# Two pre-activation layers, eight images: residual tiles reused, projection order, correlation joined by four, compact last sums

## The chip, the cores and the metric

The kernel runs on one core of a Trainium2 chip. The metric is the device time of one execution in microseconds (us). The kernel before was run three times: 2642.22, 2646.41 and 2648.47, median 2646.41.

## The reference

Eight images of 768 channels and 32x32 tokens, fp32, pass through two layers. Each layer normalizes in 32 groups of channels and adds its result to its input.

```python
def _L0_conv_ref(x, W_qkv, W_proj, b_proj):          # 12 heads of 64
    qkv = swapaxes(x.reshape(B, C, N), 1, 2) @ W_qkv.T
    q, k, v = ...
    var_v = jnp.var(v, axis=-1, ddof=1, keepdims=True)
    var_k = jnp.var(k, axis=-1, ddof=1, keepdims=True)
    scores = var_v @ jnp.swapaxes(var_k, -2, -1) * scale
    out = softmax(scores, axis=-1) @ v
    return (out as tokens x C) @ W_proj.T + b_proj

def _L1_conv_ref(feature, conv_w, conv_b):
    norm = jnp.sqrt(jnp.sum(feature * feature, axis=1, keepdims=True))
    feat_n = feature / jnp.maximum(norm, 1e-12)
    feat_pad = pad feat_n by 3 on both sides
    corr = stack of sum(feat_pad[r:h+r, cc:w+cc] * feat_n, axis=1) for 28 offsets (r, cc)
    x = jnp.concatenate([feature, corr], axis=1)       # 768 + 28 channels
    return jnp.einsum('bchw,oc->bohw', x, conv_w) + conv_b

x = x + _L0_conv_ref(_gn(x), W_qkv, W_proj, b_proj)
x = x + _L1_conv_ref(_gn(x), conv_w, conv_b)
```

The queries are not needed: the scores are an outer product of two variances for each token. The 28 offsets lie on two diagonals, a row and a column of a 7x7 window.

## The kernel before

**Products.** The three large matrix products (keys and values, projection, convolution) go by a block scheme with seven products instead of eight, numbered p = 1 to 7: some multiply sums of blocks of the weights with sums of blocks of the data. A *unit* is one such product (g, p), for one third g of the output channels: 12 matmuls of 128x64 stationary and 512 wide in the projection and the convolution (class `Wide`, 21 units each), 384 wide in keys and values (`KeysValues`). `halves` (L337 is its matmul) issues two matmuls of 64 columns for each 128 rows. All matmuls are fp32, so the trace has two passes for each instruction, and shapes like `128*64` are the tile of the array that an instruction occupies. Products 1, 5 and 2 open an accumulator in PSUM and later products add to it: `Banks.begin` opens it in one of two banks tagged x or one of two tagged y (z products use the y banks), `close` hands it to VectorE, which adds bias and residual (`take`; `vector` is a helper, and all its work stands at L153).

**Operand sums** of the data for products 5, 6/3, 7 and 4 are made by VectorE (`TokenSums`): t1, t2, t4 for layer one's output `f`, t1o, t2o, t4o for the attention output (the `ots` tiles, in the trace named v).

**Attention** (`Attention`): for each of six pairs of heads, ScalarE computes exponentials (`ex`, L738), TensorE multiplies them with the values (`av`, L763; one step of eight matmuls, 16 for half a pair in the planned order), and the denominators come either from ScalarE's running sums or from VectorE's sums `acc` of the exponentials. In the second case a product with ones (`den`) adds over partitions: `sum_up` (L797) makes four sums at once, each in a quarter of the columns, and sends them through memory to be inverted; `sum_up_last`, for an image's last pair, uses 64 columns for each sum (L847), so that the sums already lie on all 64 partitions of a head; VectorE inverts them there in four pieces and multiplies `v` with the result (v<-v,acc).

**Correlation** (`Corr`): TensorE makes grams of `f` (L1101, `gr`), of which DMAs pick the needed diagonals; `scale` turns them (`ct`, through `turned`, L340) and stores them as rows; a gather reads the rows with their shifts into `cs`, where VectorE forms the 28 channels. The channels are split like the data into two halves and their difference. They enter the convolution as a short product that is added to a unit's accumulator: `Wide.join` (L1008), which takes two units at a time, the operands of the first at partitions 0 to 39, of the second at 64 to 103. Seven images have six such joins each; for the last image the parts are added separately.

**The loop** (L1449) makes nine passes. Pass b holds the attention of image b, the second half of its keys and values, and the grams and the convolution of image b-1, interleaved; then `project(b)`, the projection of image b with the statistics for layer two; then the first half of keys and values of image b+1.

**What sets the order.** The program is emitted in one order by a planner: a clock with modelled durations (KV_US, T_US, CORR_US, TAIL and the like), `later.after(us, job)` for due times, `later.after_dve` for due times behind VectorE, and `work_off`, which mixes units and attention steps. The order on each engine is fixed by that. Nearly all DMAs are issued from SyncE (SP) in that order; an issue that waits for a reader of its target holds up those behind it. Eight completion semaphores are used in turn, so a DMA also waits until the one eight places before it has landed. Weight tiles `wt` are fetched by `TStream` (L324) up to twelve ahead (HELD).

**Residuals.** `Conv.start` loads x1 (kept in memory) into a new tile of the xn kind (x<-x1d in the trace); `project` loads x into a new tile f (L1336: f<-in_x_dram), both in six parts of 512 KB while the units already run.

The projection starts with units (0,1), (1,1), (0,5), (1,5), then products 6 and 3, whose operand t2o needs the last pair of heads. At its start stand:

```python
for n, (us, _, unit) in enumerate(wide.units()):
    if n == 4:
        clock.wait(("ot", b, HP - 1), ready=ready)
```

Of the kernel before, what the change touches and what calls it, by code (L numbers as in the profile page):

```python
# [38 lines left out]
NCH = 2 * NA + 4  # L39
# [11 lines left out]
TAIL = 14.0  # L51
# [3 lines left out]
WARM = 36  # L55
# [12 lines left out]
SINGLE = ((2, 1), (2, 5), (2, 6), (2, 2), (2, 7), (2, 3), (2, 4))  # L68
ORDER = (1, 5, 6, 3, 7, 4, 2)
OPENING = PAIR[:2] + PAIR[-2:] + PAIR[2:-2]  # L70

# [87 lines left out]
def two_layers(ctx, tc, x, wkv, wproj, bproj, wconv, wcorr, bconv, out):  # L159
# [147 lines left out]
    class TStream:  # L307
        def __init__(self):
            self.keys = []
            for b in range(NB + 1):  # L310
                for kind in ["c"] * (b > 0) + ["p"] * (b < NB):
                    some = PAIR[:-2] if b == NB - 1 and kind == "c" else PAIR
                    self.keys += [(kind, g, p) for g, p in some + SINGLE]
            at = len(self.keys) - len(PAIR + SINGLE)
            self.keys[at:at] = [("c", g, p) for g, p in PAIR[-2:]]
            self.loaded, self.tiles = 0, []
# [25 lines left out]
    class Banks:  # L342
# [8 lines left out]
        def product(self, g, p, us, width, pairs, taken):  # L351
            self.close(*self.begin(g, p, width, pairs), us, taken)

        def begin(self, g, p, width, pairs, stop=True, between=None):
            bank = BANK[p]
            of = "x" if bank == "x" else "y"
            if p in FIRST:
                slot = of, self.count[of] % 2
                self.count[of] += 1
                self.finish(slot)  # L360
                clock.pass_time(max(self.free.get(slot, 0.0) - clock.now, 0.0))
                t = (xbank if of == "x" else ybank).tile([P, width], F32, tag=of, name=f"{bank}{self.count[of]}")
                self.open[g, bank] = slot, t
            slot, t = self.open[g, bank]
            self.finish(slot)
            clock.pass_time(max(self.free.get(slot, 0.0) - clock.now, 0.0))
            for k, (lhsT, rhs) in enumerate(pairs):
                halves(
                    t, lhsT, rhs, start=p in FIRST and k == 0, stop=stop and k == len(pairs) - 1, skip_group_check=True
                )  # L370
                if between and k == 0:
                    between()
            return slot, t
# [14 lines left out]
    warm = smp.tile([P, 512], F32, tag="sm", name="warm")  # L388
    for n in range(WARM):
        nc.tensor.matmul(warm[:, 0:P], lhsT=ident, rhs=ident, start=True, stop=True)  # L390
# [53 lines left out]
    def load_corr_weights():  # L444
# [5 lines left out]
        for line, step in enumerate(STEP):  # L450
            for j in (1, 2, 3):
                n, k = AHEAD_OF.index(step * j), 3 * line + j - 1
                nc.sync.dma_start(out=wcorr_sb[n : n + 1, :, :], in_=wcorr[k : k + 1, :, :])
                nc.sync.dma_start(out=wcorr_sb[NA + n : NA + n + 1, :, :], in_=wcorr[12 + k : 13 + k, :, :])
        nc.sync.dma_start(out=wcorr_sb[2 * NA : NCH, :, :], in_=wcorr[24:28, :, :])
        nc.sync.dma_start(out=wcorr_sb[HD : HD + NCH, :, :], in_=wcorr_sb[0:NCH, :, :])

# [10 lines left out]
    class Norm:  # L468
# [7 lines left out]
        def means(self):  # L476
            name, mv = self.name, self.mv
            pm = small(f"pm{name}")
            halves(pm[:, 0:1], group_m, mv[:, 0:1])
            self.mean = st.tile([P, 1], F32, tag="mean", bufs=2, name=f"mean{name}")  # L480
# [6 lines left out]
        def spreads(self):  # L487
            name = self.name
            pv = small(f"pv{name}")
            halves(pv[:, 0:1], group_m, self.e)  # L490
            ve = st.tile([P, 1], F32, tag="ve", name=f"ve{name}")
# [216 lines left out]
    class Pair:  # L708
# [80 lines left out]

        def sum_up(self):  # L790
# [3 lines left out]
            for e in range(2):  # L794
                for hf in range(2):
                    at = 2 * e + hf
                    nc.tensor.matmul(  # L797
                        den[at * 32 : (at + 1) * 32, :], lhsT=ones[:, 0:32], rhs=self.acc[e][:, hf * HF : (hf + 1) * HF],
                        start=True, stop=True,
                    )  # L800
# [30 lines left out]
        def load_inverses(self, rows):  # L831
# [5 lines left out]
            self.rd_at = clock.now + (14.0 if (self.b, self.hp) == (1, HP // 2 - 1) else 6.0)  # L837
            self.try_finish()

        def sum_up_last(self):  # L840

            dens = []
            for hf in range(2):
                at = slice(hf * HF, (hf + 1) * HF)
                den = other([P, HF], f"den{self.b}_{self.hp}_{hf}")
                for e in range(2):
                    nc.tensor.matmul(  # L847
                        den[e * HD : (e + 1) * HD, :], lhsT=ones, rhs=self.acc[e][:, at], start=True, stop=True
                    )
                dens.append(den)  # L850
            self.rd = self.acc[0]

            def invert(n):

                q = HF // 2
                vector.reciprocal(self.rd[:, n * q : (n + 1) * q], dens[n // 2][:, n % 2 * q : (n % 2 + 1) * q])
                if n < 3:
                    later.after_dve(1.5 if self.b else 0.0, lambda: invert(n + 1))
                else:
                    self.rd_at = clock.dve  # L860
                    self.try_finish()

            later.after(1.2 if self.b else 0.0, lambda: invert(0))
# [119 lines left out]
    class Wide:  # L983
        def __init__(self, kind, name, acc, bias, operand, finished, more=None):
            self.kind, self.name, self.acc, self.bias = kind, name, acc, bias
            self.operand, self.finished, self.more, self.held = operand, finished, more, []

# [3 lines left out]
        def unit(self, g, p, between=None):  # L991
# [4 lines left out]
            if more is None:  # L996
                banks.product(g, p, T_US, HF, pairs, taken)
            else:
                self.held.append((*banks.begin(g, p, HF, pairs, stop=False, between=between), taken, *more))
                if len(self.held) == 2:  # L1000
# [3 lines left out]
        def join(self):  # L1004

            for n, (slot, t, taken, i, tokens) in enumerate(self.held):
                at = slice(n * HD, (n + 1) * HD)
# [19 lines left out]
        def units(self):  # L1027
            return [(T_US, (), lambda g=g, p=p: self.unit(g, p)) for g, p in PAIR + SINGLE]
# [40 lines left out]
    class Corr:  # L1069
# [70 lines left out]
        def scale(self, hf, dd):  # L1140
# [7 lines left out]
            def columns():  # L1148
# [4 lines left out]
                later.after_dve(0.7, lambda: to_dram(dn))  # L1153
# [19 lines left out]
        def gather(self):  # L1173
# [4 lines left out]
            nc.sync.dma_start(out=u[0:NA, :], in_=r[2:NROW, PAD : PAD + N])  # L1178
            nc.sync.dma_start(out=v[NA:NCH, :], in_=windows(r[0:1, PAD:], (0, NA + 4), (1, N)))
            nc.sync.dma_start(out=u[2 * NA : NCH, :], in_=windows(r[1:2, PAD:], (0, 4), (1, N)))  # L1180
            k = 0
            for first, _, count in RUNS:
                if not first:
                    first, count = 1, count - 1
                nc.sync.dma_start(out=v[k : k + count, :], in_=windows(r[0:1, PAD + first :], (1, count), (1, N)))
                nc.sync.dma_start(
                    out=u[NA + k : NA + k + count, :],
                    in_=windows(r[2 + k : 3 + k, PAD - first :], (ROW - 1, count), (1, N)),
                )
                k += count  # L1190

            def product():
                vector.tensor_tensor(u, u, v, ALU.mult)
                vector.tensor_tensor(cs[0:NCH, 2, :], cs[0:NCH, 0, :], cs[0:NCH, 1, :], ALU.subtract)
                nc.sync.dma_start(out=cs[HD : HD + NCH, :, :], in_=cs[0:NCH, :, :])
# [4 lines left out]
    class Conv:  # L1200


        def __init__(self, b, f, acc, after):
            self.b, self.f, self.acc, self.after = b, f, acc, after
            self.turn = False
# [3 lines left out]

        def start(self):  # L1210
            if self.acc is None:
                self.acc = image_tile(xnpool, "xn", f"x1_{self.b}")
                for n, us in ((0, 0.0), (1, 1.0), (3, 2.5), (4, 4.0), (2, 12.0), (5, 14.0)):
                    later.after(us, lambda n=n: nc.sync.dma_start(out=self.acc[:, n, :], in_=x1_dram[self.b][:, n, :]))
# [5 lines left out]
            )  # L1220
            ready.add(("acc", self.b))
# [18 lines left out]
        def units(self):  # L1240
            b, held = self.b, False
            need = {7: (("third", b),), 4: (("fourth", b),)}
            out = []
            for g, p in (PAIR[:-2] if b == NB - 2 else PAIR) + SINGLE:
                keys, us = need.get(p, ()), T_US
                if self.more(g, p):
                    keys, us, held = keys + (("cs", b),), us + CORR_US * held, not held
                out.append((us, keys, lambda g=g, p=p: self.wide.unit(g, p)))
            return out

# [22 lines left out]
        def corr(self, parts):  # L1273
# [3 lines left out]
            for n, (i, hf) in enumerate(parts):  # L1277
                at = slice(n * HD, (n + 1) * HD)
# [54 lines left out]
    def project(b, ots, held=None):  # L1333
        f = first_f[0] if b == 0 else image_tile(fpool, "f", f"f{b}")
        for n, us in ((0, 0.0), (1, 0.5), (3, 1.5), (4, 3.0), (2, 12.0), (5, 14.0)) if b else ():
# [36 lines left out]
        wide = Wide("p", f"p{b}", f, bproj_sb, sums.operand, finished)  # L1372
        late = True
        for n, (us, _, unit) in enumerate(wide.units()):
            if n == 4:
# [73 lines left out]
    for b in range(NB + 1):  # L1449
        rest, attention, ots, beside = [], None, None, []  # L1450
        if b < NB:

            ots = [v.rearrange("p t r d -> p (t r d)") for v in kv.vt]
            rest += kv.units(1)
            attention = Attention(b, kv, ots)
        if b:
            has_f = ("f", b - 1),
            if b > 1:
# [4 lines left out]
                b - 1, f, None if b < NB else acc, (lambda b=b: next_image(b + 1)) if b + 1 < NB else lambda: None  # L1463
            )
            grams = [(GRAM_US if t < MT - 1 else 0.9, has_f if b > 1 else has_f + ("turned",), lambda t=t: (corr or corrs[0]).gram(t)) for t in range(MT)]
# [70 lines left out]
```

## Time and profile before

| | us |
|---|---|
| three runs: lowest, median, highest | 2642.22, 2646.41, 2648.47 |
| the profiled execution's own time | 2640.38 |
| its span in the trace | 2638.7 |
| TensorE busy | 2610.0 |
| VectorE busy | 1604.3 |
| ScalarE busy | 1367.3 |
| GpSimd busy | 413.6 |
| DMA, mean of the 16 engines' share (first kind of queue) | 52.0% of the span |

What TensorE does, by starts of groups in the trace: exponentials times values, 3072 matmuls (two passes each), 700.2 us busy by the group's own count; the largest groups of block products are x, y and z of L337. The granted TensorE clock is full in nearly all of the span (mean 0.998).

How to read it: the timeline lists, for one engine, the start of a group of equal instructions, its length, the source line, output and inputs by name, the array tile, the shape and the count; where the engine was idle before it, the time and what released it stand in brackets. The ends of matmuls are modelled and overlap the next start, so durations are best taken from one start to the next. A unit of 12 matmuls 512 wide takes 2.58 us by starts, an attention step of eight 1.72.

### The profile page before, as it was taken

The numbers are of one execution on the slowest core, as the hardware profiler recorded it, in microseconds if no ns is written. First come the engines' busy times: TensorE is split into PE (matmuls) and PEld (weight loads), VectorE is DVE, ScalarE is ACT, GpSimd is POOL, SyncE is SP. The second block draws the span as 40 slices with busy tenths as digits, with TensorE's granted clock in tenths as the row PEclk, the third lists the DMA queues.
The fourth block names the chain that finished last, engine by engine and source line by source line (L and its number), as shares of the span: only waits on it lengthen the run. The fifth ranks groups of instructions, "written<-read, shape, count | busy, mean of one in ns | idle before, by whom it ended". The sixth has DMA issues, their size and how long they took to land.

```text
span 2638.7 us, 40466 instructions
## 1 busy us (share of the span) xinstructions
PE 2610.0 (99%) x14766; PEld 1318.2 (50%) x14766; DVE 1604.3 (61%) x4110; ACT 1367.3 (52%) x1841; POOL 413.6 (16%) x444
## 2 busy tenths in 40 slices
PE   9999999999999999999999999999999999999999
PEld 4654566334763347633476334553357433575333
DVE  5858735685447853478534885357853587535864
ACT  1498078711598116980179701897018960199500
POOL 4320130003300033000430003300133001320000
PEclk9999999999999999999999999999999999999999
DMA  7774455455553545626556265562655626545333
GB/s 285 291 247 147 144 198 158 137 182 159 188 187 113 201 153 180 198 95 214 155 172 196 87 220 158 171 205 81 221 172 154 196 84 237 169 137 164 96 117 101
DMA packets 323392, 446.65 MB, mean 169 GB/s; under 512 B 59458, under 2 KB 245170, under 8 KB 323194
## 3 DMA queue, kind: packets, MB, share of 16 engines
q1 hardware_dynamic: 321962, 441.32, 52.0%
q8 instruction: 117, 1.92, 0.3%
q10 hardware_dynamic: 1232, 2.75, 0.3%
q14 instruction: 81, 0.66, 0.1%
HBM read 377.49 MB, written 64.40 MB: 167 GB/s over the span
## 4 chain that ended last, share of the span: by engine, by line
PE 89%; DMA 3%; ACT 3%; DVE 2%; issue 1%; SPq 1%; POOL 1%; DVEq 0%; ACTq 0%; POOLq 0%
PE x L337 35%; PE av L763 22%; PE y L337 17%; PE z L337 9%; PE gr L1101 3%; ACT ex L738 1%; ACT junk L748 1%; DMA x<-x1d 1%; DMA v<-rows 1%; DMA bc<-vdr 1%; PE x L1008 1%; PE den L797 1%; PE y L1008 1%; PE z L1008 1%; DVE acc L153 1%
## 5 line engine op out<-in xcount | busy, mean ns | idle before, releaser
L738 ACT ACTIVATE ex<-bc,nk 128x1024 f32<-128x1024 f32 x768 | 828.2, 1138 | 418.7 <-DMA bc<-vdr 202.6
L763 PE MATMUL av<-ex,v 128*64 128x512 f32 x3072 | 700.2, 596 | 3.4 <-ACT ex L738 3.2
L763 PEld LDWEIGHTS av<-ex,v 128*64 128x64 f32 x3072 | 316.6, 137 | 339.0 <-issue 210.5
L748 ACT ACTIVATE junk<-bk,vm 128x1024 bf16<-128x1024 f32 x368 | 420.5, 1143 | 25.3 <-DMA bk<-kdr 15.5
L153 DVE TENSOR_TENSOR acc<-acc,ex 128x1024 f32<-128x1024 f32 x300 | 344.3, 1209 | 0.0
L215 ACT COPY kp<-x 128x384 f32<-128x384 f32 x28 | 13.4, 477 | 562.1 <-PE x L337 553.4
L337 PE MATMUL y<-kv,s 128*64 128x384 f32 x1488 | 269.4, 487 | 0.0
L337 PE MATMUL x<-kv,xn 128*64 128x384 f32 x1512 | 264.3, 489 | 1.6 <-DVE xn L153 1.6
L337 PE MATMUL x<-kv,s 128*64 128x384 f32 x1488 | 258.2, 486 | 0.0
L337 PEld LDWEIGHTS x<-kv,xn 128*64 128x64 f32 x1512 | 145.3, 138 | 101.1 <-issue 80.5
L337 PEld LDWEIGHTS x<-kv,s 128*64 128x64 f32 x1488 | 145.2, 137 | 91.2 <-issue 67.6
L337 PEld LDWEIGHTS y<-kv,s 128*64 128x64 f32 x1488 | 140.7, 137 | 87.1 <-issue 69.2
L494 POOL TENSOR_TENSOR rstda<-vea,neghalf 128x1 f32<-128x1 f32 x8 | 4.8, 595 | 964.4 <-DVE vea L153 964.4
L1086 POOL TENSOR_TENSOR turn<-f,ones 128x384 f32<-128x384 f32 x112 | 110.9, 1010 | 248.3 <-PE gr L1101 167.6
L337 PE MATMUL z<-kv,xn 128*64 128x384 f32 x768 | 135.1, 486 | 0.0
L337 PE MATMUL x<-v,wt 128*64 128x512 f32 x576 | 131.1, 594 | 0.0
L337 PE MATMUL x<-f,wt 128*64 128x512 f32 x504 | 120.1, 594 | 0.0
L153 DVE TENSOR_TENSOR v<-y,v 128x128 f32<-128x128 f32 x180 | 40.9, 282 | 127.3 <-PE y L337 127.3
L600 POOL TENSOR_TENSOR s<-xn 128x384 f32<-128x384 f32 x64 | 66.8, 1052 | 287.2 <-PE x L337 199.0
L153 DVE BATCH_NORM_STATS2 vbn<-v 128x6 f32<-128x64 f32 x720 | 101.6, 209 | 0.0
L337 PEld LDWEIGHTS z<-kv,xn 128*64 128x64 f32 x768 | 76.4, 137 | 45.9 <-issue 34.3
L1101 PEld LDWEIGHTS gr<-f,turn 128*64 128x64 f32 x1344 | 88.3, 137 | 13.2 <-issue 5.2
(192 smaller groups left out, 3006.5 us busy)
## 6 DMA issues: line engine op xcount, KB each, us to landing
kv<-kvs SPq DMA_DIRECT2D x124, 576.0 KB
kv<-in_wkv_dram SPq DMA_DIRECT2D x95, 576.0 KB
bc<-vdr SPq DMA_DIRECT2D x96, 512.0 KB
f<-in_x_dram SPq DMA_DIRECT2D x48, 512.0 KB
bk<-kdr SPq DMA_DIRECT2D x46, 512.0 KB
x1d<-f SPq DMA_DIRECT2D x42, 512.0 KB
x<-x1d SPq DMA_DIRECT2D x42, 512.0 KB
out_dram<-x SPq DMA_DIRECT2D x82, 256.0 KB
```

The lines of the kernel that those rows point to most:

```text
L153: return getattr(self.engine, name)(*args, **kw)
L215: nc.scalar.copy(to, at)
L337: nc.tensor.matmul(out[at], lhsT=lhsT[:, at], rhs=rhs, start=start, stop=stop, **kw)
L494: nc.gpsimd.tensor_tensor(self.rstd, ve, neghalf[:, 0:1], ALU.pow)
L600: nc.gpsimd.tensor_tensor(self.sums[g][:, 0], a[g][2], a[g][3], ALU.add)
L738: nc.scalar.activation(ex, self.bc[e], AF.Exp, scale=self.kv.nk[self.half][:, h, t : t + 1])
L748: nc.scalar.activation(junk, self.bk[e], AF.Exp, scale=self.kv.m2[self.half][:, h, t : t + 1], accum_out=self.sums[:, e, t : t + 1],)
L763: nc.tensor.matmul(self.av[e * HD : (e + 1) * HD, hf, :], lhsT=self.vt[:, t, e, :], rhs=exs[e][:, hf * HF : (hf + 1) * HF], start=t == 0, ...
L797: nc.tensor.matmul(den[at * 32 : (at + 1) * 32, :], lhsT=ones[:, 0:32], rhs=self.acc[e][:, hf * HF : (hf + 1) * HF], start=True, stop=True,)
L1008: nc.tensor.matmul(t, lhsT=wcorr_sb[at, i, :], rhs=cs[at, tokens, :], start=False, stop=True, skip_group_check=True)
L1086: nc.gpsimd.tensor_tensor(to[:, :, side], half, windows(ones, ones.ap[0], (0, J), (HW, 4), (1, HW)), ALU.mult)
L1101: nc.tensor.matmul(ps[side * HD : (side + 1) * HD, :n].rearrange("p (y x) -> p y x", x=WIDE), lhsT=block[:, j, side, :], rhs=image[:, 4 * ...
```

## The change

1. The correlation channels are kept compact (28 rows instead of 40) and laid at four partition quarters; `cs` is copied three times instead of once, and the gather has 14 DMAs instead of 11. Joins take four units for the first two of each image but the last two, then two; the order of the convolution's units follows (`QUADS`), and unit (0,2) is then accumulated in an smp bank (`apart`).
2. The projection's order (`LOWS`) begins with six units that need only the first pairs of heads; the x and y accumulators of the third are in an av tile (`home`). The planner's wait for the last pair moves from the fourth to the sixth unit, TAIL from 14 to 8.
3. `sum_up_last` makes four sums at once in 32 columns each, as `sum_up` does; VectorE inverts them in two pieces on 128 partitions; eight DMAs inside SBUF (64 KB each, four from SP, four from ScalarE's queue) copy them to all 64 partitions of each head.
4. The residual of the convolution is loaded into the tile of image b's normalized data, the low thirds before the last units of keys and values read the rest; the residual of the projection goes into the tile `f` of the image before, the low thirds near the end of the convolution.
5. For image 0 the correlation's `to_dram` (the turn `ct`) is due 5.0 us after its scaling instead of 0.7.
6. 42 warm matmuls instead of 36 at the start, 6 and 12 more between the first statistics products, in an av bank. The due time of loaded inverses is 8 us instead of 6.

```diff
-NCH = 2 * NA + 4
+PICKED = ((1, 1), (31, 1), (62, 2), (93, 3))
+CHANNELS = [first + apart * n for first, apart in PICKED for n in range(3)]
+NS = len(CHANNELS)
+NCH = 2 * NS + 4
-TAIL = 14.0
+TAIL = 8.0
-WARM = 36
+WARM, BRIDGE = 42, (6, 12)
+QUADS = PAIR[:10] + ((0, 2),) + PAIR[10:12] + ((1, 2), (2, 5), (2, 1)) + SINGLE[2:]
+FOUR = P // 4
+LOWS = ((0, 1), (2, 1), (1, 1), (0, 5), (1, 5), (2, 5)) + PAIR[4:] + SINGLE[2:]
+def conv_order(b):
+    return QUADS if b < NB - 2 else (PAIR[:-2] if b == NB - 2 else PAIR) + SINGLE
...
+            if apart:
+                t = other([P, width], f"{bank}{g}")
...
-            if p in FIRST:
+            if p in FIRST and home and bank in home:
+                self.open[g, bank] = ("home", bank), home[bank]
+            elif p in FIRST:
...
-    for n in range(WARM):
-        nc.tensor.matmul(warm[:, 0:P], lhsT=ident, rhs=ident, start=True, stop=True)
+    keep_warm(WARM)
...
+            if name == "a0":
+                keep_warm(BRIDGE[0])
...
+        def ones_products(self, den):
+            for at in range(4):
+                e, hf = divmod(at, 2)
+                nc.tensor.matmul(
+                    den[at * 32 : (at + 1) * 32, :], lhsT=ones[:, 0:32], rhs=self.acc[e][:, hf * HF : (hf + 1) * HF],
+                    start=True, stop=True,
+                )
...
         def sum_up_last(self):
+            den = other([P, HF], f"den{self.b}_{self.hp}")
+            self.ones_products(den)
+            self.rd, rc = self.acc[0], self.acc[1][:, 0:HF]
+            q = HF // 2
             def invert(n):
+                vector.reciprocal(rc[:, n * q : (n + 1) * q], den[:, n * q : (n + 1) * q])
+                later.after_dve(0.5, spread if n else lambda: invert(1))
+            def spread():
+                for at in range(4):
+                    e, hf = divmod(at, 2)
+                    to = self.rd[e * HD : (e + 1) * HD, hf * HF : (hf + 1) * HF]
+                    rows = rc[at * 32 : (at + 1) * 32, :]
+                    for half in range(2):
+                        (nc.scalar if e else nc.sync).dma_start(out=to[half * 32 : (half + 1) * 32, :], in_=rows)
+                self.rd_at = clock.now + 5.0
+                self.try_finish()
+            later.after(1.7 if self.b else 1.0, lambda: invert(0))
...
-                if len(self.held) == 2:
+                if len(self.held) == (self.joined[0] if self.joined else 2):
+                    self.joined = self.joined[1:]
                     self.join()
...
-                at = slice(n * HD, (n + 1) * HD)
+                at = slice(n * FOUR, n * FOUR + NCH)
...
-            return [(T_US, (), lambda g=g, p=p: self.unit(g, p)) for g, p in PAIR + SINGLE]
+            return [(T_US, (), lambda g=g, p=p: self.unit(g, p)) for g, p in LOWS]
...
-                later.after_dve(0.7, lambda: to_dram(dn))
+                later.after_dve(0.7 if b else 5.0, lambda: to_dram(dn))
...
-                nc.sync.dma_start(out=cs[HD : HD + NCH, :, :], in_=cs[0:NCH, :, :])
+                for n in range(1, 4):
+                    nc.sync.dma_start(out=cs[n * FOUR : n * FOUR + NCH, :, :], in_=cs[0:NCH, :, :])
...
+        def low_residual(self):
+            self.early = True
+            for n in range(JH):
+                later.after(1.5 * n, lambda n=n: self.residual(n))
         def start(self):
-            if self.acc is None:
-                self.acc = image_tile(xnpool, "xn", f"x1_{self.b}")
-                for n, us in ((0, 0.0), (1, 1.0), (3, 2.5), (4, 4.0), (2, 12.0), (5, 14.0)):
-                    later.after(us, lambda n=n: nc.sync.dma_start(out=self.acc[:, n, :], in_=x1_dram[self.b][:, n, :]))
+            if self.early:
+                for n, us in ((3, 0.0), (4, 1.5), (5, 8.0)):
+                    later.after(us, lambda n=n: self.residual(n))
...
+            self.wide.joined = [4, 4] if self.b < NB - 2 else []
...
     def project(b, ots, held=None):
-        f = first_f[0] if b == 0 else image_tile(fpool, "f", f"f{b}")
-        for n, us in ((0, 0.0), (1, 0.5), (3, 1.5), (4, 3.0), (2, 12.0), (5, 14.0)) if b else ():
+        f = first_f[0] if b == 0 else layer1[b - 1][0]
+        for n, us in ((3, 0.0), (4, 1.5), (5, 8.0)) if b else ():
...
+        own = avp.tile([P, 2, HF], F32, tag="av", name=f"own{b}")
+        wide.home = {"x": own[:, 0, :], "y": own[:, 1, :]}
...
-            if n == 4:
+            if n == 6:
                 clock.wait(("ot", b, HP - 1), ready=ready)
...
+            if b:
+                rest.insert(len(rest) - 5, (0.0, (), lambda: conv.low_residual()))
```

## The prediction

> **What bounds the kernel now.** I read the busy times first, then what TensorE waits for, then its timeline by stage.
>
> ```profile
> span 2638.7 us, 40466 instructions
> PE 2610.0 (99%) x14766; PEld 1318.2 (50%) x14766; DVE 1604.3 (61%) x4110; ACT 1367.3 (52%) x1841; POOL 413.6 (16%) x444
> ```
>
> TensorE is busy 99% of the span, so an edit counts only as work taken from it, or as a stall given to it or taken from it. Its waits (total us, times, longest) are few:
>
> ```profile
> PE x L337 <- DVE x L153: 4.6, 6, 0.9
> PE ct L340 <- DVE dn L153: 3.3, 1, 3.3
> PE av L763 <- ACT ex L738: 3.2, 2, 2.4
> ```
>
> VectorE's 52 us of waiting for residual loads (26.1 for f, 26.2 for x1d) are not among them: taking those away is worth nothing by itself. The profiled run took 2640.38 us, 6.0 (0.2%) under the median of the runs, 2646.41; I sum against the profiled run and add 6.0. A measurement of this kernel can tell about 0.2%, 5 us, from no change.
>
> **Joins by four.** In TensorE's timeline (start, us) a join of today is four matmuls: two row groups of 64 partitions at once, two passes.
>
> ```profile
> 800.18 2.74 PE L337 MATMUL y<-f,wt 128*64 128x512 f32 x12
> 802.86 0.69 PE L1008 MATMUL x<-cs,wcorr_sb 64*128 64x512 f32 x1
> 802.86 0.69 PE L1008 MATMUL y<-cs,wcorr_sb 64*128 64x512 f32 x1
> ...
> 803.91 7.09 PE L763 MATMUL av<-ex,v 128*64 128x512 f32 x32
> ```
>
> The first two start together, the second pass (left out here) 0.53 later, the next work at 803.91. A unit of 12 matmuls lasts 12 x 0.2146 = 2.58, so this join and its switches took 803.91 - 800.18 - 2.58 = 1.15; over all 42 that difference averages 1.24. Six images go from six pairs to two quads and two pairs: 12 joins fewer. No row shows four row groups. If they run at once, a quad costs a pair's time, and 12 x 1.24 = 14.9 goes; if only two at a time, a quad costs a second 1.06 and 12 x (1.24 - 1.06) = 2.2 goes. The nearest row is the four column groups of L797, eight matmuls in 1.00 (below), so I take 14.9. A rule speaks against it: the Trainium skill, "TensorEngine Tiling (Array Packing)", Gotcha 1, says that different row tiles can't access one PSUM bank at the same time. The quad's four outputs lie in four banks (two x, two y, or for the second quad an smp bank in place of one), so by it too the sum is 14.9; two in one bank would make it 2.2. No trace here shows the conflict.
>
> The second quad's product (0,2) sits in an smp bank; den3_3 finds the other free, so nothing waits. The correlation operands need 14 gather DMAs and three copies instead of 11 and one, five more on SP at about 0.5 us of issue, behind which weight fills queue. I cost them at nothing: weight tiles are fetched twelve ahead (some 30 us), and TensorE waited for one for 1.6 us in the whole span. With that cover gone each late tile costs up to 2.5.
>
> **Compact last sums.**
>
> ```profile
> 824.22 1.06 PE L797 MATMUL den<-acc,ones 128*32 128x512 f32 x8
> 825.22 7.09 PE L763 MATMUL av<-ex,v 128*64 128x512 f32 x32
> ...
> 874.27 1.94 PE L847 MATMUL den<-acc,ones 128*64 128x512 f32 x8
> 876.04 2.74 PE L337 MATMUL y<-f,wt 128*64 128x512 f32 x12
> 879.51 2.79 PE L337 MATMUL x<-t4f,wt 128*64 128x512 f32 x12 [0.72 <-DVE x L153]
> ```
>
> Four groups at once take 1.00 from start to next start, two 1.77. Eight images: 8 x 0.77 = 6.2 off. Two reciprocals instead of four (1.74 each) take 3.5 us from VectorE in front of an x that TensorE wants: that is the third stall above, seen at 879.51. By starts, 879.51 - 876.04 - 2.58 = 0.9, in six images; the shorter stream, and half an attention step put between, remove it: -5.6 (0 if x is still late).
>
> **The price of it: the spread.** The inverses must now be copied over partitions by eight DMAs, four on SP, four on ACT (idle there). Call D the end of the den matmuls. Today, with D = 876.04 (two rows of VectorE, one of TensorE):
>
> ```profile
> 890.48 1.23 DVE L153 TENSOR_TENSOR v<-v,acc 128x1024 f32<-128x1024 f32 x1
> 891.62 1.89 DVE L153 TENSOR_TENSOR t2o<-v,t1o 128x512 f32<-128x512 f32 x3
> ...
> 893.65 5.32 PE L337 MATMUL x<-t2o,wt 128*64 128x512 f32 x24
> ```
>
> The product is in time by about 1 us. After, the six products that need no late tile cover 6 x 2.58, so TensorE wants t2 at D+15.5. In SP's order for images 2 to 6 the four spreads stand behind weight fills that wait for the second, third and fourth of these products (D+5.15, +7.73, +10.3) and behind the 512 KB load of f; with a fill's and a load's 0.55 each they issue at D+11.4 to D+12.9. Landing is bounded by the rows of other small and large transfers, 1.15 (den<-ds) to 8.5 (xn<-in_x, median); I take windowed<-win, 2.35, as the nearest in size: D+15.2. Then 1.23 for the mult, 0.68 for the first t2: D+17.2, a stall of 1.7 (0.5 to 7.8) in five images: +8.7 (2.5 to 39). For image 0 (19.3 us of work after its sums) and 1 (25 us) there is cover, for 7 no f load stands ahead: nothing. VectorE's queue behind the mult holds the takes of the next products; they are late by the same amount, no more.
>
> **Residuals and order.** The low thirds of x1 and f go into tiles whose readers in TensorE and GpSimd stand before them; SP's issue waits there for the last of them, in the planned order at most one key or value unit (1.93) away, in front of weight fills with the lead told above. So nothing, and if that lead is lost 1.9 an image. Moving loads out of the projection's start relieves the DMA engines, which were 95% busy from 885 to 910; that speaks for a quick spread.
>
> **Single stalls of image 0.**
>
> ```profile
> 395.70 0.44 PE L340 MATMUL ct<-ident,dn 128*64 128x128 f32 x4 [3.33 <-DVE dn L153]
> 395.94 3.37 PE L763 MATMUL av<-ex,v 128*64 128x512 f32 x8
> 399.03 1.88 PE L1101 MATMUL gr<-f,turn 128*64 128x133 f32 x24
> ...
> 396.00:400.00 4.00, 4.00 (x23) 2.00 (x21) 0.29 (x1) 4.00 (x6) 0.00 (x0) 0.57 0.06 14
> ```
>
> The last line is a window of the trace, its 0.57 the granted clock. The wait costs 3.3 idle (3.7 by starts); then the granted clock falls to half for 3.41 us (0.57 over four us), and eight av matmuls take 3.09 instead of 1.72: 5.4 in all. The longer delay moves ct0_0 behind that whole av1_1: -5.4. Of the clock, the Trainium skill ("TensorE: Matmul & The Clock Gate", Part 1) says that the gate halves after an idle window of about 3.4 us; here 3.33 and, at 477.70, 2.45 of idling sufficed, and the row decides. By the page, stalls under 3.4 would cost only themselves.
>
> Three smaller ones: the den0_4 wait (64 av matmuls from 228.51 should end at 242.3; den starts at 244.43 and lasts 2.19 instead of 1.00) is filled with key and value units: -3.4. The t2o wait of image 0 (288.74, 1.62 idle, 2.4 by starts) goes with the shorter chain: -2.4. At the start 6 and 12 warm matmuls (0.112 each) delay pva by 0.45 and the first key unit by 1.3, against 24 matmuls at half clock today (5.6 instead of 3.9): -0.4 (-1.7 to +1.5). The wait for ex at 477.70 (2.45, then half clock) has one join less before it while ScalarE's chain is unchanged: +0.6 (-5.9 to +1.3).
>
> **Sum.** -14.9 - 6.2 - 5.6 - 5.4 - 3.4 - 2.4 - 0.4 + 0.6 = -37.7; +8.7 makes -29.0. 2640.4 - 29.0 = 2611.4, and at the median's level 2617.4.
>
> **Rivals.**
>
> A. The spread lands midway, some 5 us after issue: a stall of 4.3 each, more than the 2.45 that halved the clock, so another 1.7 each: 5 x 6.0 = 30. -37.7 + 30 = -8: 2639. For it: spreads issue late by SP's order; f<-in_x takes 6.8 in the median. Against: 64 KB, and three loads fewer there.
>
> B. Quads run two at a time: 12.7 of the joins' gain is missing, -16: 2630. For it: no row with four row groups. Against: L797.
>
> C. Slower. The spreads stand in the DMA engines behind f's and the next image's 512 KB loads and take xn<-in_x's 8.5: each of the five images stalls 7.8 and loses 1.7 at half clock: 47.5, -37.7 + 47.5 = +10: 2656. It decides from 37.7/5 = 7.5 per image on, landing past D+19.3. For it: the 95% busy stretch, weight fills up to 8.6. Against: xn loads stood at D+15.9 to D+21 today, after the spreads' place.
>
> D. It doesn't do what it says: quads not formed, or weight tiles late, so that the gains of the image-0 stalls alone pay the spread: about 2646. The planned order shows twelve quads, so little speaks for it. The planner's other constants (TAIL, the due times of inverses) show only through this order.
>
> **How the numbers follow.** Forecast 0.60 (its own range 2606 to 2629, from -40 with a spread at 0.5, to -17), A 0.12, B 0.12, C 0.14, D 0.02. The time is the forecast's. The range goes from 2604, where the start and the wait at 477.70 also come out well, to 2640, which takes in A and B and leaves C and the upper part of A. Faster by over 0.2%: 0.60 + 0.12 + 0.07 of A = 0.79; within: 0.03 of A and D = 0.05; slower: C and 0.02 of A = 0.16.
>
> **What would show it.** Quads: four matmuls of 32x512 starting together, next work 1.1 to 1.3 after the unit before; 2.1 is B. TensorE's waits: x from DVE t2o five times 1 to 3 us is the forecast, 4 and more with a granted clock of half after it A, 8 is C. Gone should be ct from dn, x from x, and L847. A wait of TensorE for wt or cs, or VectorE in front of an x product, would make the prediction wrong in a way not listed.

## The result and the profile after

The changed kernel takes 2659.05 us in the median of five runs (2655.69 to 2660.47); the kernel before, with two more runs beside these, 2642.22 (2640.07 to 2648.47). The ratio is 1.0056, 95% interval 1.0040 to 1.0072: slower by about 15 us (16.8 between the medians), where 29 less was forecast, and outside the range.

The page of the changed kernel's profiled run (2660.47 us) and, below the dots, TensorE's waits (total us, times, longest):

```profile
span 2658.7 us, 40713 instructions
PE 2605.5 (98%) x14814; PEld 1361.2 (51%) x14814; DVE 1576.7 (59%) x4094; ACT 1367.2 (51%) x1841; POOL 414.9 (16%) x444
...
PE x L347 <- DVE t2o L164: 18.9, 6, 4.8
PE own L347 <- DVE f L164: 15.6, 14, 1.7
PE x L347 <- DVE xn L164: 4.8, 1, 4.8
```

TensorE is busy for 4.5 us less than before, and x from x and ct from dn are gone as forecast; but the three waits shown stand in their place, 39 us of idling in all (before, t2o and xn had one wait of 1.6 each). The second kind, of products into `own`, the av tile with the accumulators of the projection's third pair, is not in the prediction.

Where the time went is seen by cutting both traces at the first product of each projection and the first key product after it, up to the start of the last group of matmuls:

| stretch | before, us | after, us | difference |
|---|---|---|---|
| start to projection 0 | 275.8 | 275.1 | -0.7 |
| projection 0 | 57.0 | 55.6 | -1.4 |
| first key product to projection 1 | 226.6 | 215.8 | -10.8 |
| the same to projections 2 to 6 | 1349.1 | 1325.8 | -23.3 |
| projections 1 to 6 | 6 x 54.36 | 380.7 | +54.5 |
| the rest | 397.0 | 399.3 | +2.3 |

Everything outside projections 1 to 6 brought 34 us, near the 37.7 of the sum. Projections 1 to 6 cost 54.5, where 8.7 was put down. Image 2's projection on TensorE (start, us; in brackets the idle time and its releaser):

```profile
874.15 1.07 PE L820 MATMUL den<-acc,ones 128*32 128x512 f32 x8
875.15 2.79 PE L347 MATMUL x<-v,wt 128*64 128x512 f32 x12
...
888.08 2.74 PE L347 MATMUL own<-t1o,wt 128*64 128x512 f32 x12
894.56 7.93 PE L347 MATMUL x<-t2o,wt 128*64 128x512 f32 x24 [3.74 <-DVE t2o L164]
902.33 2.74 PE L347 MATMUL y<-v,wt 128*64 128x512 f32 x12
...
923.13 2.77 PE L347 MATMUL own<-t2o,wt 128*64 128x512 f32 x12
925.74 2.74 PE L347 MATMUL own<-v,wt 128*64 128x512 f32 x12
929.34 2.79 PE L347 MATMUL own<-v,wt 128*64 128x512 f32 x12 [0.86 <-DVE f L164]
931.96 2.75 PE L347 MATMUL z<-v,wt 128*64 128x512 f32 x12
936.41 2.80 PE L347 MATMUL own<-t4o,wt 128*64 128x512 f32 x12 [1.71 <-DVE f L164]
```

The t2o products start 3.9 us late and then need 7.77 (to 902.33) instead of 5.15, since the granted clock is half from 892.9 to 899.8. Later two own products wait 1.02 and 1.87 by starts. VectorE says why (start, us):

```profile
888.29 0.75 DVE L164 SCALAR_TENSOR_TENSOR f<-y,bproj_sb,f 128x512 f32<-128x512 f32 x1 [1.82 <-PE y L347]
892.68 1.23 DVE L164 TENSOR_TENSOR v<-v,acc 128x1024 f32<-128x1024 f32 x1 [3.63 <-DMA acc<-acc]
893.82 1.89 DVE L164 TENSOR_TENSOR t2o<-v,t1o 128x512 f32<-128x512 f32 x3
...
924.73 0.80 DVE L164 TENSOR_SCALAR xn<-xn,meana,rstda 128x1024 f32<-128x1024 f32 x1
928.53 0.75 DVE L164 SCALAR_TENSOR_TENSOR f<-own,bproj_sb,f 128x512 f32<-128x512 f32 x1 [3.01 <-PE own L347]
```

At 892.68 it had waited for the spread. At 928.53 it takes product (2,6), which TensorE finished at 925.7, only after (2,3), in the other half of the same PSUM tile, ends: its wait goes by the tile and lasts until the newest write to either half (the first experiment tests this). TensorE's (2,7) then waits for this take. By starts, images 2 to 6 lose 19.4 to t2o and 10.9 to half clock; image 1 loses 5.0 and 2.6; the own waits are 15.9 in images 1 to 6: 53.8 of the 54.5.

In image 1 the multiplication stands in VectorE's order in front of two takes of the convolution (VectorE's timeline):

```profile
540.82 0.68 DVE L164 TENSOR_TENSOR xn<-x,xn 128x512 f32<-128x512 f32 x1
552.31 1.23 DVE L164 TENSOR_TENSOR v<-v,acc 128x1024 f32<-128x1024 f32 x1 [10.81 <-DMA acc<-acc]
553.45 1.89 DVE L164 TENSOR_TENSOR t1o<-v 128x512 f32<-128x512 f32 x3
555.26 0.68 DVE L164 TENSOR_TENSOR xn<-z,xn 128x512 f32<-128x512 f32 x1
555.86 0.74 DVE L164 SCALAR_TENSOR_TENSOR xn<-x,bconv_sb,xn 128x512 f32<-128x512 f32 x1
```

VectorE idles 10.81 us in front of it, and TensorE's third projection product waits 4.82 at 556.66 for a bank that the take at 555.86 frees.

The quads themselves work (TensorE's timeline):

```profile
794.63 2.90 PE L347 MATMUL y<-f,wt 128*64 128x512 f32 x12
797.46 0.69 PE L1038 MATMUL y<-cs,wcorr_sb 28*128 28x512 f32 x1
797.46 0.70 PE L1038 MATMUL x<-cs,wcorr_sb 28*128 28x512 f32 x2
797.48 1.10 PE L1038 MATMUL y<-cs,wcorr_sb 28*128 28x512 f32 x2
...
798.53 2.79 PE L347 MATMUL z<-f,wt 128*64 128x512 f32 x12
```

Eight matmuls (four outputs, two passes) take 798.53 - 797.46 = 1.07, where a pair takes 1.06; the switch in front of a quad is 0.28 in the mean, where that of a pair was 0.18 before. With twelve joins fewer, joins and switches take 13.9 us less of TensorE.

### The profile page after: what moved, and what is told of

Same layout as the page of the kernel before. It is cut to its first block, busy times and chain, and to the rows that moved or that the text cites. A ratio compares the mean times of both kernels' runs of the same rounds, so it can differ in the third digit from the quotient of the medians.

```text
span 2658.7 us, 40713 instructions
## 1 busy us (share of the span) xinstructions
PE 2605.5 (98%) x14814; PEld 1361.2 (51%) x14814; DVE 1576.7 (59%) x4094; ACT 1367.2 (51%) x1841; POOL 414.9 (16%) x444
## 3 DMA queue, kind: packets, MB, share of 16 engines
q10 hardware_dynamic: 2768, 4.85, 0.5%
## 4 chain that ended last, share of the span: by engine, by line
PE 92%; DVE 3%; DMA 3%; SPq 1%; issue 1%; ACT 0%; POOL 0%; DVEq 0%; ACTq 0%; POOLq 0%
PE x L347 33%; PE av L789 24%; PE y L347 16%; PE z L347 9%; PE own L347 4%; PE gr L1131 3%; DMA acc<-acc 1%; PE den L820 1%; DMA wt<-tsp 1%; DVE xn L164 1%; DVE f L164 1%; PE y L1038 1%; DVE acc L164 0%; PE z L1038 0%; SPq L886 0%
## 5 line engine op out<-in xcount | busy, mean ns | idle before, releaser
L789 PEld LDWEIGHTS av<-ex,v 128*64 128x64 f32 x3072 | 333.2, 137 | 318.1 <-issue 182.7
L164 DVE TENSOR_TENSOR v<-v,rd 128x1024 f32<-128x1024 f32 x40 | 48.7, 1218 | 101.4 <-DMA rd<-di 79.8
```

The source lines that it names most:

```text
L164: return getattr(self.engine, name)(*args, **kw)
L789: nc.tensor.matmul(self.av[e * HD : (e + 1) * HD, hf, :], lhsT=self.vt[:, t, e, :], rhs=exs[e][:, hf * HF : (hf + 1) * HF], start=t == 0, ...
```

## The experiments

All times are medians; the ratio is to the kernel before, run beside each, with its 95% interval. Landings of DMAs are read from their completion semaphores in the trace. The expectations stand as they were put down ahead of the runs.

**The shared tile.** The av bank pair as two tiles:

```diff
-own = avp.tile([P, 2, HF], F32, tag="av", name=f"own{b}")
-wide.home = {"x": own[:, 0, :], "y": own[:, 1, :]}
+own = [avp.tile([P, HF], F32, tag=f"av{n}", name=f"own{b}_{n}") for n in range(2)]
+wide.home = {"x": own[0], "y": own[1]}
```

> The changed kernel with its av bank pair made of two PSUM tiles instead of one tile with two halves (everywhere: attention, the last image's parts, the projection's third pair); order and work unchanged. Theory: the 14 waits of TensorE for f before an own product (18.6 us by starts) come from VectorE's take of one half waiting for products in the other half of the same tile, so they go and nothing else does: about 2641 us, the t2o waits still 3 to 5 us in five images. Rival: VectorE is behind because t2o came late, and the own waits follow from that: then they stay and the time stays at 2659.

Measured: 2640.51, ratio 0.9983 (0.9973 to 0.9993). Its waits:

```profile
PE x L347 <- DVE t2o L164: 19.2, 6, 4.6
PE x L347 <- DVE xn L164: 4.8, 1, 4.8
PE av L789 <- ACT ex L764: 2.7, 2, 1.4
```

The own waits are gone and the others untouched: the two losses are separate, and the shared tile cost 18.5 us by the medians (19.4 by the spans of the profiled runs).

**The old last sums in the changed kernel**: `sum_up_last` as before the change.

> The changed kernel with the last sums as in the kernel before (two den products of 64 columns, four reciprocals in place, no spread DMAs). Theory: the t2o waits (19.4 us in images 2 to 6), the half clock after them (10.9) and image 1's stall behind the multiplication (7.6 with its half clock) all come from the eight spread DMAs landing late; they go, 6.2 of den time comes back: about 2659 - 31.7 = 2627 us, own waits stay at 15 to 19. Rival: the six products are too short a cover whatever brings the inverses (four reciprocals take 7 us of VectorE): t2o waits of 2 us or more stay, 2640 or above.

Measured: 2634.51, ratio 0.9964 (0.9951 to 0.9977). The t2o waits of images 2 to 7 and image 1's stall are gone, own waits stay at 15.6. The 7 us above the expectation are mostly one new wait of image 0 (4.0 from 290.9, and 1.75 at half clock after it), whose four reciprocals end later (at 288.8, against 283.5 before the change).

**Both edits.**

> Both edits together. Theory: the two losses are separate, so they add: about 2659 - 18.6 - 31.7 = 2609 us, 33 under the kernel before, each projection about 55 us from its first product to the first key product as before. Rival (one loss causes the other, or VectorE becomes the bound in the projection): 2620 or more.

Measured: 2616.62, ratio 0.9896 (0.9881 to 0.9911): the two gains, 18.5 and 24.5, add. It is 7.6 above the expectation and under the rival's 2620; image 0's wait is in this run too. Projections 2 to 6 last 54.5, against 54.4 before the change.

**Joins of two**, in the convolution order of before:

```diff
-self.wide.joined = [4, 4] if self.b < NB - 2 else []
+self.wide.joined = []
-    return QUADS if b < NB - 2 else (PAIR[:-2] if b == NB - 2 else PAIR) + SINGLE
+    return (PAIR[:-2] if b == NB - 2 else PAIR) + SINGLE
```

> The changed kernel with joins of two units only, in the convolution order of before (operands still compact at the partition quarters). Theory: twelve joins of 1.06 plus a switch come back, 12 x 1.24 less twelve times what a quad's switch costs more (0.1): about +13.7, 2673 us. Rival: the quads' order had cost as much in waits as it saved: 2659 to 2663.

Measured: 2631.48, ratio 0.9953 (0.994 to 0.9965): 28 us faster with more work, and both expectations missed. The timeline of TensorE in image 2:

```profile
863.81 1.06 PE L820 MATMUL den<-acc,ones 128*32 128x512 f32 x8
864.81 2.80 PE L347 MATMUL z<-f,wt 128*64 128x512 f32 x12
867.43 2.75 PE L347 MATMUL x<-t4f,wt 128*64 128x512 f32 x12
...
871.16 2.79 PE L347 MATMUL x<-v,wt 128*64 128x512 f32 x12
...
886.67 5.32 PE L347 MATMUL x<-t2o,wt 128*64 128x512 f32 x24
```

With this order the planner puts the last sums in front of two convolution units and their join instead of behind them: 6.4 us more cover (864.81 to 871.16). The spread is no faster (the multiplication starts at 883.29, 18.5 after the sums, against 17.5 in the changed kernel), but now it is in time. Projections 1 to 6 take 41.9 us less than in the changed kernel (t2o and half clock, image 1's stall, and half of the own waits, 8.4 against 15.6), the stretches in front of them 13.3 more.

**TAIL 14 instead of 8**, quads kept, gives the sums that place.

> The changed kernel with one planner constant put back, TAIL 14 instead of 8: from image 2 on the last den stands in front of the last two units of the convolution and their join, as it does with joins of two, instead of behind them; cover for the spread 6.4 + 15.5 us. Theory: the spread is late because its cover was planned away, not because of the quads themselves: t2o waits of images 2 to 6 and the half clock after them (30 us) go, the own waits shrink as they did with pairs (8 instead of 16), image 1's stall of 7.6 stays: about 2659 - 30 - 7 = 2622 us. Rival: quads cost by themselves (their four held banks, later cs, DMA load), so it stays above 2640 although pairs had 2631.

Measured: 2640.4, ratio 0.9987 (0.9977 to 0.9996). 18 above the theory's figure and at the edge of the rival's, but not by the rival's cause. No t2o wait is left among the listed, but the own waits did not shrink (16.4, 19 times, longest 2.4): the take of (2,1) stands behind the late multiplication in VectorE's order, and (2,5), in the same tile, waits for it (1.15, 1.43, 2.59, 1.84 and 1.83 by starts in images 2 to 6). So part of the lateness came back through the shared tile. And each stretch from the first key product to projections 2 to 6 takes 267.1 instead of 265.2, that to projection 1 1.5 more: the longer tail has a price of its own, 11 us.

**All spreads on ScalarE's queue.**

```diff
-(nc.scalar if e else nc.sync).dma_start(out=to[half * 32 : (half + 1) * 32, :], in_=rows)
+nc.scalar.dma_start(out=to[half * 32 : (half + 1) * 32, :], in_=rows)
```

> The changed kernel with all eight spread DMAs on ScalarE's queue, none behind SP's weight fills and loads. Theory: they are issued from 881.6 to 886.5 in image 2 instead of up to 889.1 and land about 2 us sooner; the t2o stall falls from 3.9 to about 2 and TensorE keeps its full clock: five times 2 + 2.2 = 21 us less, 2638. Rival (the DMA engines' load decides, not the queue): landing as late as before, 2655 to 2659.

Measured: 2676.54, ratio 1.0118 (1.0101 to 1.0135): the opposite of the expectation. Image 2's DMA issues, SP and then ScalarE's queue:

```profile
882.45 0.62 SPq L1380 DMA_DIRECT2D f<-in_x_dram  x1
883.16 5.25 SPq L222 DMA_DIRECT2D xn<-in_x_dram  x6
...
878.78 5.66 ACTq L886 DMA_DIRECT2D acc<-acc  x8
```

The sums end at 870.4 here. ScalarE issues from 8.4 to 14.0 us after that, hardly sooner than SP's last in the changed kernel (14.5), since the second reciprocal ends 2 us later and eight issues take 5.66 on one queue. And SP, freed of its four, issues the next image's 512 KB loads at 883.16, in front of the last two spreads. The first six spreads landed 2.3 to 3.7 us after issue, the last two (883.28, 883.84) after 5.9 and 7.1, at 891.0: 20.6 after the sums instead of 17.3. The t2o stalls of images 2 to 6 are 6.4 to 7.7. What shares the DMA engines decides; these stalls are the price that rival C named.

**TAIL 14 and split tiles**, compact sums kept:

> TAIL 14 and the av bank pair as two tiles, everything else as changed (quads, compact sums, early residuals). Theory: the losses are the lost cover and the shared tile, and both are mended: no t2o waits in images 2 to 7 and no own waits, image 1's 7.6 stays: about 2622 - 11 = 2611 us, under the kernel with both earlier edits (2616.6) by the den time of 6. Rival: the compact sums are still paid in the projection: 2617 or more.

Measured: 2622.5, ratio 0.9915 (0.9899 to 0.9931): 11 above the expectation, most of it the longer tail's price: 267.1 instead of 265.2 with the split alone in each of the five stretches to projections 2 to 6. Image 1's stall (4.85 and 2.6) is the largest left.

**Old sums, split tiles, TAIL 14:**

> Old last sums, split tiles and TAIL 14. Theory: images 2 to 7 had no t2o stall left in the kernel with both edits, so only image 0's wait (4.0 and 1.75 at half clock) goes: 2616.6 - 5.7 = 2611 us. Rival: the longer tail takes units from between attention steps and av waits for ex come up: 2617 or more.

Measured: 2615.79, ratio 0.989 (0.9874 to 0.9906). Image 0's wait is gone, but each stretch from the first key product to the next projection takes 267.2 instead of 265.9: the rival's price, by another way than ex.

**The quads alone**: joins of two in the kernel with both edits.

> The kernel with old last sums and split tiles (2616.6), joins of two only. Here no spread is left that their order could cover, so the quads are seen alone. Theory: twelve joins come back, 12 x 1.24 less 12 x 0.1 of switch: +13.7, 2630 us. Rival (the quads cost by themselves what joins of two showed against the changed kernel): 2616 or less.

Measured: 2626.41, ratio 0.993 (0.9917 to 0.9942): the quads are worth 10 us by the medians, 12.3 by the spans of the profiled runs (2626.9 and 2614.6). So in the changed kernel they brought their gain, and the 28 that joins of two were faster by are waits that their order does not have.

**The longer tail in the first pass only:**

> The kernel with old last sums and split tiles, with the tail of 14 in the first pass alone. Theory: image 0's t2o wait (4.0 and 1.75 at half clock) goes and the longer tail's price in the other passes (1.3 a pass, by the time from one key product to the next projection's start in the two kernels) is not paid: 2611 us. Rival: the first pass pays the same in its attention: 2615 to 2617.

Measured: 2609.94, ratio 0.9865 (0.985 to 0.9881). This beats both kernels: 1.35% under the one before. Its granted clock is full up to the last matmul.

**Residuals at the times of before**, into the reused tiles:

> The kernel with old last sums and split tiles, with the residuals loaded at the stages' starts as in the kernel before (six parts each at 0 to 14 us), still into the reused tiles. Theory: VectorE waits for them, TensorE does not: 2616.6 plus 0 to 3. Rival: with the shorter projection their takes now come too late and TensorE waits for x and y banks: 2625 or more.

Measured: 2693.19, ratio 1.0182 (1.0166 to 1.0198): 77 us worse. Its waits:

```profile
PE x L347 <- DVE v L164: 17.6, 5, 4.0
PE ptv L350 <- DVE vm L164: 16.8, 5, 3.8
PE x L347 <- DVE t2o L164: 13.2, 7, 3.6
```

VectorE waits 73.9 us for f, and what stands behind those takes (v sums, vm, t2o) comes late. The run does not separate two causes: the loads' old times fit the old order, and the new order takes the third part of f, due at 12 us, with its second unit. It shows that early loads are a condition of this order, not that they gain by themselves.

**Compact sums with image 1 mended**, by a later due time of its inverses:

```diff
-self.rd_at = clock.now + 5.0
+self.rd_at = clock.now + (12.0 if self.b == 1 else 5.0)
```

> The kernel with TAIL 14 and split tiles (2622.5, compact sums kept), with image 1's multiplication by the inverses placed four takes and three sums later in VectorE's order, TensorE's order unchanged. Theory: image 1's stall (4.85 and 2.6 at half clock) comes from VectorE standing in front of that multiplication while the spread's DMAs land, with two takes of x banks behind it; it goes: 2622.5 - 7.5 = 2615 us. With no stall of the spread left the compact sums then show their net worth beside the same kernel with the old sums (2615.8): 0, where the den rows alone say 6. Rival: the stall moves to t2o, 2620 or more.

Measured: 2616.2, ratio 0.99 (0.9884 to 0.9917). Image 1's stall is gone, and the compact sums are level with the old ones (2615.79). Its trace shows where part of the 6 us of den time goes: x from xn 2.1 us in six waits, and two waits of 1.5 and 0.9 for wt in images 3 and 4 (1.67 and 1.02 by starts). Why weights come late there was not tried.

## Why the prediction was wrong

**Right: the gains.** Summed over the stretches outside projections 1 to 6 they were 34, where the terms gave 37.7. Joins: 14.9 forecast, 13.9 by the rows. Den: 1.00 us each as forecast. The six x stalls and the ct wait are gone (0.4 left of ct), and so is the half clock at 396.3 and 478.2; the wait for ex in front of the second went from 2.45 to 1.25, where +0.6 stood. Image 0's t2o wait went too. The den0_4 wait is gone but for 0.2, but its den stays slow (2.12 instead of 1.00): about 2 of 3.4. The start gained nothing: the first z product is at 22.66 instead of 22.49. Of the 6.0 added for the level of the median, 1.8 held: with five runs the median before is 2642.22, and the profiled run took 2640.38.

**Wrong: "The price of it: the spread".** The cover, 6 x 2.58, was right (the wait begins at 890.7, D+15.5 with D = 875.15). The last spread was issued at D+13.9 instead of 12.9, and landed 3.35 after it, not 2.35; the ScalarE four, issued from 881.58, took 4.8 to 5.7. That makes D+17.3 for the last landing instead of 15.2, and a stall of 3.2 to 4.9 each instead of 1.7. The price taken for the landing was the median of the 34 KB transfers; these spreads shared the DMA engines with f's loads. In image 0, where the DMA share is 0.48 from 279.7 to 288.0 (0.87 in image 2 from 881.5 to 892.4), the eight took 1.98 to 2.96, so the 2.35 fits a quiet stretch. And a stall of this size brings half clock, which the forecast's 1.7 had no term for and rival A had: A's 6.0 an image is what was measured, 30.3 in all.

**Wrong: "For image 0 ... and 1 (25 us) there is cover".** The cover of t2o was counted, not what is queued behind the multiplication on VectorE: two takes, one of which frees a bank that TensorE needs before t2o. The sentence that these takes are late "by the same amount, no more" put nothing down for that bank; the stall was 5.0, and 2.6 at half clock. The run with that multiplication moved shows it: 6 us less (2622.5 to 2616.2).

**Missing: the third pair's tile.** The forecast put no cost on the x and y accumulators lying in one av tile. The split run gives it: 18.5. The order of waits could have been read beforehand, since (2,6) and (2,3) follow each other in that tile, and (2,7) needs the take of the first.

**The rivals.** C's time (2656) came out near the measured one, but by another sum: its landing of 8.5 was only come near, with all spreads on ScalarE's queue (7.1 in image 2), where the time was 2676.5. B and D are refuted by the quads' rows. The early residuals cost nothing as forecast, but "nothing" hid that the new order depends on them.

The Trainium skill ("DMA: Bandwidth & Descriptors", "Issuing engines are not separate DMA queues") says that DMAs of all issuing engines run on the same 16 engines, and that issuing from several saves only the time of issue. The run with all spreads on ScalarE's queue agrees: its last two took 5.9 and 7.1 us beside SP's loads, the six ahead of those 2.3 to 3.7.

## What to carry to other kernels

A moved step that turns in-place work into DMAs has to be priced with the transfers that share its microseconds, and with every instruction queued behind its consumer, not only with the engine that waits for its result. An accumulator pair in one tile made a take of one half wait for the products of the other, 18.5 us here: give halves that are used in turn tiles of their own. When a new order or a shorter tail moves a step in a planned program, look at what stood behind the step as cover: with the tail of 8, the quads' order, worth 10 us of joins, put the last sums behind two units and their join, and 6.4 us of cover went in each image.

## What was not expected of the hardware

The granted clock went to half after TensorE had idled 2.42 us (image 4 in the run with TAIL 14, from 1540.7), as it had after 2.45 in the kernel before, and not after 1.67 in images 5 and 6 of that run. These windows of the trace (us, TensorE busy, other engines, granted clock, DMA share, GB/s) show the changed kernel around image 2's stall:

```profile
888.00:892.00 4.00, 2.82 (x14) 0.72 (x10) 0.75 (x1) 0.00 (x0) 0.00 (x0) 1.00 0.86 233
892.00:894.00 2.00, 0.00 (x0) 0.00 (x0) 1.32 (x2) 0.00 (x0) 0.00 (x0) 0.73 1.01 379
894.00:898.00 4.00, 3.44 (x8) 1.00 (x10) 2.37 (x4) 0.00 (x0) 0.00 (x0) 0.50 1.02 415
```

All periods at half clock in the changed kernel last 3.413 us or twice that: 6.83 in images 1, 2 and 4, 3.41 in 3, 5 and 6, so a stall of 3.2 to 4.9 costs 1.7 to 3.05 more. Their starts lie whole multiples of 3.413 apart (555.01 and 892.93: 99; before the change, 396.27 and 478.19: 24), as if the clock were decided window by window on a fixed grid. Cut by that grid, the 14 traces have 39 windows at full clock, behind the first 26 us, in which TensorE idled 2.12 us or more: each is followed by half clock. In none of the others did it idle more than 1.96, and none of them is. So what counts in these traces is how much of a stall falls into one window: of the 3.02 idle in front of image 6's t2o products, 2.28 did. A window at half clock is followed by another when TensorE idled 0.75 or more in it (1.64, 1.63 and 0.75 in images 1, 2 and 4), and never with 0.63 or less.

The Trainium skill ("TensorE: Matmul & The Clock Gate", Part 1) gives windows of 3413 ns, which agrees, and a fall after at least one idle window; here 2.12 of 3.41 us idle were enough, and the measurement decides.
